# Dividing the attention's output without transposes: sums on sixteen rows of each head

## The chip, the core and the metric

The kernel runs on one core of a Trainium2 chip. The metric is the device time of one execution in microseconds (us); less is better. A core has five engines with a queue of instructions each: TensorE (PE, matmuls and transposes; its weight loads are listed as PEld), VectorE (DVE), ScalarE (ACT), GpSimd (POOL) and SyncE (SP, which here only starts DMA transfers). Each engine works through its queue in order. TensorE writes to PSUM, a memory of eight banks with 128 partitions of 2 KB each (512 numbers of 32 bits); VectorE and ScalarE read PSUM and write to the on-chip memory SBUF or back to PSUM.

## The reference, cut to what matters

The model has two layers on x of 8 batches x 256 tokens x 256 features: a correlation attention, a mixture of experts with balanced assignment, a cross attention, and a mixture with two experts per token. The change is in the cross attention and in what follows it at once:

```
q = (x @ Wq + bq).reshape(bs, n_ctx, HEADS, d)
kv = (data @ Wkv + bkv).reshape(bs, n_data, HEADS, 2 * d)
k, v = (kv[..., :d], kv[..., d:])
scores = jnp.einsum('bqhd,bkhd->bhqk', q, k) * scale
attn = jax.nn.softmax(scores, axis=-1)
out = jnp.einsum('bhqk,bkhd->bqhd', attn, v).reshape(bs, n_ctx, WIDTH)
return out @ Wp + bp
...
x = x + _L1_xattn_ref(_layernorm(x, axis=-1), ctx_1024, L1_xattn_Wq, ...)
x = x + _L1_ffn_ref(_layernorm(x, axis=-1), L1_ffn_gate_W, ...)
```

The softmax is computed as exponents first, sums of the exponents beside the product with v, and a division at the end.

## The kernel before, in words

Everything is in 32-bit floats. The program order of every engine's queue is written out by hand: what `fast_path` calls first is first in the queues. Work of several batches is interleaved, so that TensorE always has something to do.

**The attention stage** (`for b in range(B): for c in range(NB):`, L3018 to L3107) runs over 8 batches b and two halves c of 8 heads. Per half it issues `scores` for two tiles of 128 keys (L2666): four matmuls of 32 rows each, one per pair of heads, where `QM` holds the queries of a pair twice, once with the first head's features kept and once with the second's (m = 0, 1). Two exponents on ScalarE follow (L2681). `values` (L2685) then multiplies the exponents of the half before (`prev`) with `VA`: for each head a block of 32 columns, 16 of v, one of ones, 15 of zeros. So each head has 32 rows of the result `pv`: 16 features, one row with the sum of the exponents, 15 of nothing.

From there to the projection there are five steps. `keep` (L2698) copies pv to SBUF on VectorE. `turn_back` (L2702) turns both halves of a batch with eight transposes on TensorE, so that tokens lie on partitions and the sum of a head is a column; VectorE takes the reciprocal of 16 sums per token and multiplies (L2717, L2718). `turn_out` (L2725) turns the normalised output back with four transposes, and VectorE copies it (L2735). `project_out` (L2737) multiplies with Wp and VectorE adds to X (L2749).

Around it: `turn_q` (L2628) turns the normalised rows of the next batch but one, VectorE copies them (`hT`); `queries` (L2632) computes the queries of a batch in two halves c, each with its own PSUM tile `pp`, and makes the two masked copies m with the mask `mask[:, m]`: m = 0 on ScalarE, m = 1 on VectorE. `norm_q` normalises the rows for turn_q, `batch_stats` takes mean and variance (VectorE, with a power on POOL), `add_y` adds the expert output of the layer before, `add_bias` runs on POOL. For the mixture that follows, the rows of batch b-2 are normalised by POOL (`norm_m`) and turned: for batches 0 to 5 by `take_apart_m` (ScalarE splits the numbers into 16-bit halves, two DMA transposes on SP's queue turn them) and `join_m` (ScalarE), for the last two batches by `turn_m` (four transposes on TensorE, a copy on ScalarE). The router (`route`, L2843) is a generator, advanced step by step from batch 4 on by `next(gates)`; its small products (`pl`, `pt`, `pc`) use the same PSUM tiles.

PSUM in this stage: the pool `ps_m` has three tiles of one bank, used in turn by pt, pp, pl and pc; `ps_s` has two tiles of two banks for scores; `ps_v` has one bank for pv. A tile that comes round again waits until the last reader of its former content is done.

After the loop (L3767 to L3827) the last values, turn_back, turn_out and project_out are placed between pieces of the shared expert's first matmuls (`classic_up`, L3237). From L3885 on the mixture runs in units of a seven-product scheme, whose sums of operands (`Rows.steps`, four VectorE operations) are placed at fixed points of `run_unit` (`early`, `amid`, `late`, `after`).

Of the kernel before, what the change touches and what calls it, by code (L numbers as in the profile page):

```python
# [9 lines left out]
F32 = mybir.dt.float32  # L10
# [1076 lines left out]
def fast_path(  # L1087
# [263 lines left out]
    KT = pk.tile([P, NB, T], F32, name="KT")  # L1351
    VA = pk.tile([P, NT, H, HW], F32, name="VA")
    WK = pst.tile([P, KC, H, DH], F32, name="WK")
# [61 lines left out]
    def vals(i, n, pool, copy=nc.scalar.copy):  # L1415
        pp = pool.tile([P, n, H, DH], F32, tag="pm", name="pp")
        for j in range(n):
            for kc in range(KC):
                nc.tensor.matmul(
                    pp[:, j],  # L1420
                    CT[:, kc, (i + j) * P : (i + j + 1) * P],
                    wkv[:, kc, :, 1, :],
                    start=(kc == 0),
                    stop=(kc == KC - 1),
                )
                if kc < KC - 1 or j < n - 1:
                    yield
        copy(VA[:, i : i + n, :, 0:DH], pp)
        yield
# [65 lines left out]
    nc.vector.tensor_copy(bsel, fold.to_broadcast([P, NCT, 16]))  # L1495
    nc.gpsimd.memset(VA[:, :, :, DH:], 0.0)
    nc.gpsimd.memset(VA[:, :, :, DH : DH + 1], 1.0)

# [965 lines left out]
    for e in range(E - 1):  # L2464
        if e == 5:

            wpv = L1_xattn_Wp.rearrange("(c g m d) n -> m g d c n", c=NB, g=4, m=2)
            for m in range(2):
                for g in range(4):
                    r0 = 64 * m + DH * g  # L2470
                    nc.sync.dma_start(out=wp[r0 : r0 + DH], in_=wpv[m, g])
                    nc.sync.dma_start(
                        out=bvc[r0 : r0 + DH, :],
                        in_=bkv[:, 1, :].rearrange("(c g m) d -> m g d c", c=NB, g=4)[m, g],
                    )
            nc.sync.dma_start(out=bpb, in_=L1_xattn_bp.partition_broadcast(P))
        search(
            e, rows.get(e), steps_of(e), *FILLS.get(e, (2.58, [2.58] * 4))
        )
        if e < 2:  # L2480
            for k, _ in enumerate(listers[e]):
                fill((1.29, 0.43, 1.72, 0.43)[k])
# [59 lines left out]
    banks = ctx.enter_context(ExitStack())  # L2542
    ps_m = banks.enter_context(tc.tile_pool(name="ps_m", bufs=3, space=PSUM))
    ps_s = banks.enter_context(tc.tile_pool(name="ps_s", bufs=2, space=PSUM))
    ps_v = banks.enter_context(tc.tile_pool(name="ps_v", bufs=1, space=PSUM))
    pq2 = at.enter_context(tc.tile_pool(name="pq2", bufs=2))
# [15 lines left out]

    QM, hTs, h2s, norms = {}, {}, {}, {}

# [67 lines left out]
    def queries(b, c, eng=nc.scalar):  # L2632
        if c == 0:
            QM[b] = pq2.tile([P, NB, 2, S], F32, tag="QM", name="QM")
        pp = ps_m.tile([P, S], F32, tag="pm", name="pp")
        for kc in range(KC):
# [7 lines left out]
        for m in range(2):  # L2644
            if m == 0 and eng is nc.scalar:
                nc.scalar.activation(
# [16 lines left out]
    pex = at.enter_context(tc.tile_pool(name="pex", bufs=4))  # L2663
    ex, pvs, ovs, ons, oTs = {}, {}, {}, {}, {}

# [19 lines left out]
    def values(b, c, m):  # L2685
        if m == 0:
            pvs[b, c] = ps_v.tile([P, 2, S], F32, tag="pv", name="pv")
        for kt in range(TPB):
            for g in range(4):
                nc.tensor.matmul(  # L2690
                    pvs[b, c][32 * g : 32 * g + 32, m, :],
                    VA[:, b * TPB + kt, 8 * c + 2 * g + m, :],
                    ex[b, c, kt][:, g, m, :],
                    start=(kt == 0),
                    stop=(kt == TPB - 1),
                )

    def keep(b, c):  # L2698
        ovs[b, c] = pxs.tile([P, 2, S], F32, tag="ov", name="ov", bufs=3)
        nc.vector.tensor_copy(ovs[b, c], pvs.pop((b, c)))  # L2700

    def turn_back(b):  # L2702

        on = pxs.tile([P, TPB, NB, 2, 4, DH], F32, tag="on", name="on")
        ons[b] = on
        for qt in range(TPB):
            pt = ps_m.tile([P, NB, 2, 4, HW], F32, tag="pm", name="pt")
            for c in range(NB):
                for m in range(2):
                    nc.tensor.transpose(  # L2710
                        pt[:, c, m].rearrange("p g w -> p (g w)"),
                        ovs[b, c][:, m, qt * P : (qt + 1) * P],
                        ident,
                    )
            pv = pt.rearrange("p c m g w -> p (c m g) w")
            rs = small.tile([P, H, 1], F32, tag="rs", name="rs")
            nc.vector.reciprocal(rs, pv[:, :, DH : DH + 1])  # L2717
            nc.vector.tensor_tensor(  # L2718
                on[:, qt].rearrange("p c m g d -> p (c m g) d"),
                pv[:, :, 0:DH],  # L2720
                rs.to_broadcast([P, H, DH]),
                ALU.mult,
            )

    def turn_out(b):  # L2725
        pt = ps_m.tile([P, NB, TPB, P], F32, tag="pm", name="pt")
        for c in range(NB):
            for qt in range(TPB):
                nc.tensor.transpose(
                    pt[:, c, qt, :],  # L2730
                    ons[b][:, qt, c].rearrange("p m g d -> p (m g d)"),
                    ident,
                )
        oTs[b] = pxs.tile([P, NB, TPB, P], F32, tag="oT", name="oT")
        nc.vector.tensor_copy(oTs[b], pt)  # L2735

    def project_out(b):  # L2737
        pp = ps_m.tile([P, TPB, D], F32, tag="pm", name="pp")
        for qt in range(TPB):
            for c in range(NB):  # L2740
                nc.tensor.matmul(
                    pp[:, qt, :],
                    oTs[b][:, c, qt, :],
                    wp[:, c, :],
# [12 lines left out]
    def turn_m(b):  # L2757
# [3 lines left out]
            nc.scalar.copy,  # L2761
        )

    def between_m(b, kc):
        return HT[:, kc, (b + 1) * S : (b + 3) * S].bitcast(U16)

    def take_apart_m(b):  # L2770
        parts = between_m(b, 0)
        nc.scalar.copy(
            parts.rearrange("p (r t d) -> p r t d", r=TPB, t=2),
            HP[:, TPB * b : TPB * (b + 1), 0:D]
            .bitcast(U16)
            .rearrange("p r (d t) -> p r t d", t=2),
        )
        turned = between_m(b, 1).rearrange("p (c q) -> p c q", q=S)
        for r in range(TPB):
            nc.sync.dma_start_transpose(  # L2780
                out=turned[:, :, r * P : (r + 1) * P],
                in_=parts[:, 2 * D * r : 2 * D * (r + 1)],
            )

    def join_m(b):
        nc.scalar.copy(
            HT[:, :, b * S : (b + 1) * S]
            .bitcast(U16)
            .rearrange("p k (q t) -> p k q t", t=2),
            between_m(b, 1).rearrange("p (t k q) -> p k q t", t=2, k=KC),  # L2790
        )
# [226 lines left out]
    for b in range(B):  # L3018
        for c in range(NB):
# [4 lines left out]
            if (b, c) == (3, 0):  # L3024
                router_weights()
            if prev:
                values(*prev, 0)
                values(*prev, 1)
                keep(*prev)
            send()  # L3030
            if prev is None:
                list(vals(4, 1, ps_m, nc.vector.tensor_copy))
            elif b == 0:
                turn_q(1)
            elif c == 0:
                if b + 1 < B:
                    turn_q(b + 1)
            else:
                turn_out(b - 1)
                if b >= 2:  # L3040
                    take_apart_m(b - 2)
            if c == 0 and b >= 3:
                join_m(b - 3)
            if gates:
# [14 lines left out]
            if c == 0:  # L3059
                if b >= 1:  # L3060
                    turn_back(b - 1)
                if 0 < b and b + 1 < B:
# [705 lines left out]
    values(*prev, 1)  # L3768
    keep(*prev)
    join_m(B - 3)  # L3770
    at.close()
# [6 lines left out]
    next(up0)  # L3778
    turn_back(B - 1)
    gate2 = route(2)  # L3780
    next(gate2)
    next(up0)
    turn_out(B - 1)
    next(gate2)
# [3 lines left out]
    norm_m(B - 1)  # L3788
    send(2)
    next(gate2)  # L3790
    turn_m(B - 2)
# [34 lines left out]
    for do in shared.steps(P, HF):  # L3826
# [6 lines left out]
        for i in range(2)  # L3833
    ]
    ps_a = ctx.enter_context(tc.tile_pool(name="ps_a", bufs=2, space=PSUM))
    ps_e = ctx.enter_context(tc.tile_pool(name="ps_e", bufs=2, space=PSUM))
    ps_m = ctx.enter_context(tc.tile_pool(name="ps_m", bufs=1, space=PSUM))
    ps_v = ctx.enter_context(tc.tile_pool(name="ps_v", bufs=1, space=PSUM))
# [47 lines left out]
    for b in range(NBLK):  # L3886
# [24 lines left out]
        for k in range(1, NK):  # L3911
# [18 lines left out]
            if b == 1 and k == 3:  # L3930
                t = turned[n]
                early, amid = [lambda: t.join(0)], [lambda: t.join(1)]
                xs_[n] = Rows(t.RT)
                after = xs_[n].steps()
            if b == 2 and k == 1:
                amid = [lambda: t.join(0), lambda: t.join(1)]
                xs_[n] = Rows(t.RT)
            if b == 2 and k == 2:
                late = xs_[n].steps()
            run_unit(up_unit(b, k), early, amid, late, after)  # L3940
# [72 lines left out]
```

## Time and profile before

| what | us |
|---|---|
| median of 3 runs | 808.18 (807.61 to 808.23) |
| the profiled execution | 807.99 |
| its span, first to last instruction | 806.3 |
| TensorE busy in the span | 790.3 (98%) |
| mean granted TensorE clock | 0.997 |
| attention stage (205 to 360): PE, DVE, ACT, POOL busy of 155 | 152.1, 98.4, 97.5, 72.7 |

The profile is of one execution. A group line names the line of the code, the engine, the operation, the output and inputs by their names in the program, and how often it ran. The timeline gives start and duration in us; in brackets stands the time for which the engine had been idle and the instruction that released it. "Busy" of TensorE has modelled ends, so consecutive groups overlap by some hundredths in the timeline; the time from one start to the next is what a piece of work takes in the queue.

### The profile page before, as it was taken

Reading aid. Unit: us, or ns where it says so; the run is one execution under the profiler, and the core shown is the slowest. Engines: PE = TensorE matmul, PEld = TensorE weight load, DVE = VectorE, ACT = ScalarE, POOL = GpSimd, SP = SyncE. Lnnn points to the kernel's source line nnn. Section 1 sums busy time; section 2 is a strip of 40 time slices with the busy share of each in tenths; the row PEclk is TensorE's granted clock in tenths of the full one; section 3 lists DMA queues with packets and bytes.
Section 4 is the critical chain, followed back from the end, with each engine's and each line's share of the span. In section 5 each row is a group of like instructions: output and inputs, shape, how many; then the busy total and the mean of one; then the engine's idle time right before and its main releaser. Section 6 shows DMA issues by size and latency. Waiting matters only on the chain. (4 is left out here: it accounts for less than half of the span.)

```text
span 806.3 us, 13762 instructions
## 1 busy us (share of the span) xinstructions
PE 790.3 (98%) x5100; PEld 627.6 (78%) x5100; DVE 521.1 (65%) x1473; ACT 369.6 (46%) x676; POOL 214.2 (27%) x293
## 2 busy tenths in 40 slices
PE   7999999999999999999999999999999999999997
PEld 6547778788755555547898989798979898999996
DVE  6367887640466686456866686767676859686732
ACT  4344455234367777531425364444444535433430
POOL 6343122231126546543230001102122311112030
PEclk9999999999999999999999999999999999999999
DMA  8292666596161102161113585797759554411023
GB/s 267 78 307 86 218 202 174 191 269 224 53 182 30 27 16 59 41 210 60 56 55 100 170 243 156 190 298 197 196 137 296 111 179 112 122 14 20 8 30 132
DMA packets 111252, 111.16 MB, mean 138 GB/s; under 512 B 32936, under 2 KB 101768, under 8 KB 111144
## 3 DMA queue, kind: packets, MB, share of 16 engines
q1 hardware_dynamic: 102504, 96.87, 39.9%
q0 software_dynamic: 7920, 13.02, 7.6%
q8 instruction: 42, 0.69, 0.4%
q10 hardware_dynamic: 752, 0.30, 0.1%
q14 instruction: 34, 0.28, 0.1%
HBM read 80.61 MB, written 25.37 MB: 131 GB/s over the span
## 5 line engine op out<-in xcount | busy, mean ns | idle before, releaser
L3589 POOL DMA_INDIRECT Od<-Y,ids x32 | 50.7, 1584 | 285.1 <-DVE Y L3414 100.0
L3274 ACT COPY B<-a 128x512 f32<-128x512 f32 (+1 forms) x54 | 28.6, 531 | 168.2 <-PE a L3286 132.2
L2681 ACT ACTIVATE ex<-p,scale 128x1024 f32<-128x1024 f32 x64 | 67.8, 1110 | 25.3 <-PE p L2673 24.5
L3286 PE MATMUL a<-T,HP 128*128 128x256 f32 x288 | 73.9, 379 | 0.0
L3136 DVE TENSOR_TENSOR cc<-e,s 128x512 f32<-128x512 f32 x44 | 30.4, 691 | 57.1 <-PE e L3286 57.0
L3286 PE MATMUL a<-RT,wab 128*128 128x256 f32 x256 | 66.4, 382 | 0.4 <-DVE cc L3136 0.4
L3136 DVE TENSOR_TENSOR act<-act 128x256 f32<-128x256 f32 (+1 forms) x120 | 61.5, 513 | 2.7
L2385 PE MATMUL ph<-RT,w 128*128 128x256 f32 x256 | 62.0, 390 | 0.0
L2402 PE MATMUL py<-w,A 128*128 128x256 f32 x256 | 61.6, 387 | 0.0
L3286 PEld LDWEIGHTS a<-T,HP 128*128 128x128 f32 x288 | 54.0, 190 | 7.0
L3286 PEld LDWEIGHTS a<-RT,wab 128*128 128x128 f32 x256 | 46.5, 190 | 8.1 <-issue 1.6
L2385 PEld LDWEIGHTS ph<-RT,w 128*128 128x128 f32 x256 | 45.1, 190 | 8.0 <-ACT RT L2370 0.5
L2402 PEld LDWEIGHTS py<-w,A 128*128 128x128 f32 x256 | 46.3, 190 | 6.1
L2394 ACT ACTIVATE A<-ph,b1c 128x256 f32<-128x256 f32 x64 | 30.3, 474 | 43.7 <-PE ph L2385 36.7
L2944 POOL DMA_INDIRECT Td<-HP,to x32 | 32.6, 1017 | 59.5 <-DMA Td<-HP,to 54.1
L2673 PE MATMUL p<-QM,KT 32*128 32x512 f32 x256 | 41.0, 639 | 1.0 <-DVE QM L2654 0.5
L3136 DVE TENSOR_TENSOR act<-act,cc 128x512 f32<-128x512 f32 x44 | 30.3, 689 | 13.2 <-ACT act L3320 13.0
L2412 POOL DMA_INDIRECT Yd<-Y,ids x16 | 15.8, 988 | 74.5 <-DVE Y L2411 22.5
L3301 ACT COPY s<-a 128x512 f32<-128x512 f32 x44 | 25.8, 587 | 20.0 <-PE a L3286 20.0
L3286 PE MATMUL e<-T,wab 128*128 128x256 f32 x128 | 32.9, 380 | 0.3 <-DVE T L3136 0.3
L3136 DVE TENSOR_TENSOR cc<-a,s 128x512 f32<-128x512 f32 x44 | 30.4, 691 | 3.9
L3286 PE MATMUL B<-RT,wab 128*128 128x256 f32 x128 | 32.9, 379 | 0.0
(522 smaller groups left out, 1732.4 us busy)
## 6 DMA issues: line engine op xcount, KB each, us to landing
w<-in_L_ffn_w_dram SPq DMA_DIRECT2D x16, 1024.0 KB
wab<-in_L_ffn_w_e_dram SPq DMA_DIRECT2D x16, 1024.0 KB
wc<-in_L_ffn_w_e_dram SPq DMA_DIRECT2D x8, 1024.0 KB
sab<-in_L_ffn_w_e_dram SPq DMA_DIRECT2D x32, 256.0 KB
R<-Td SPq DMA_DIRECT2D x8, 530.0 KB
sc<-in_L_ffn_w_e_dram SPq DMA_DIRECT2D x16, 256.0 KB
Td<-blank SPq DMA_DIRECT2D x2, 1590.0 KB
X<-in_x_dram SPq DMA_DIRECT2D x4, 512.0 KB
```

The costliest lines, as they stand in the source:

```text
L2385: nc.tensor.matmul(ph, w1[:, kc, f * P : (f + 1) * P], RT[:, kc, :], start=(kc == 0), stop=(kc == KC - 1),)
L2394: nc.scalar.activation(A[:, f, :], ph, AF.Gelu_apprx_tanh, bias=b1c[:, e, f : f + 1])
L2402: nc.tensor.matmul(py, A[:, f, r * P : (r + 1) * P], w2[:, f, :], start=(f == 0), stop=(f == NF - 1),)
L2412: nc.gpsimd.indirect_dma_start(out=Yd, out_offset=bass.IndirectOffsetOnAxis(ap=ids[:, r : r + 1], axis=0), in_=Y[:, r, :], in_offset=None,)
L2673: nc.tensor.matmul(ps[g // 2][:, g % 2].rearrange("p m q -> p (m q)"), KT[rows, c, k0 : k0 + P], QM[b][rows, c].rearrange("p m q -> p (m q)"),
L2681: nc.scalar.activation(e4[:, 2 * j : 2 * j + 2], ps[j], AF.Exp, scale=scale)
L2944: nc.gpsimd.indirect_dma_start(out=Td, out_offset=bass.IndirectOffsetOnAxis(ap=to[g][:, k, j : j + 1], axis=0), in_=HP[:, GT * g + j, :], ...
L3136: eng.tensor_tensor(out, a, b, op)
L3274: nc.scalar.copy(self.b[:, 0 : self.n], self.a[:, 0 : self.n])
L3286: nc.tensor.matmul(ps[:, m * HT2 : (m + 1) * HT2], self.w.get(m, left, self.k), self.x.part[right], start=start and m == 0, stop=True, ski ...
L3301: nc.scalar.copy(self.s2, self.a)
L3589: nc.gpsimd.indirect_dma_start(out=Od, out_offset=bass.IndirectOffsetOnAxis(ap=ids, axis=0), in_=Y, in_offset=None, compute_op=ALU.add,)
```

## The change

`VA` now holds, for each pair of heads, four blocks of 16 columns: v of the first head, ones, ones, v of the second. `values` takes blocks 0 and 1 for m = 0 and blocks 2 and 3 for m = 1. So in the 32 rows of a pair, pv[:, 0] has the first head's features on rows 0 to 15 and its sum on each of rows 16 to 31; pv[:, 1] has the second head's sum on rows 0 to 15 and its features on rows 16 to 31. keep, turn_back and turn_out are gone; `divide` takes their place: it gathers the sums in `den`, swaps the 16-row halves, inverts, gathers the features in pv[:, 0], and multiplies. Its result already has features on partitions, as project_out needs them; the rows of Wp are loaded in the new order.

pv comes from `ps_m`, which has two tiles now; `ps_s` has three. The two halves of a batch's queries share one tile. Of the four masked copies ScalarE makes three (both of c = 1). turn_q stands ahead of values. The mixture's rows of all batches go through `turn_m`, at half c = 1 of the second next batch; `take_apart_m` and `join_m` are gone. Some sums of `Rows` are placed later, and the pools of the last stage are opened in another order.

```
-    VA = pk.tile([P, NT, H, HW], F32, name="VA")
+    VA = pk.tile([P, NT, H // 2, 4, DH], F32, name="VA")
...
-    nc.gpsimd.memset(VA[:, :, :, DH:], 0.0)
-    nc.gpsimd.memset(VA[:, :, :, DH : DH + 1], 1.0)
+    nc.gpsimd.memset(VA[:, :, :, 1:3, :], 1.0)
...
-                    r0 = 64 * m + DH * g
+                    r0 = 2 * DH * g + DH * m
...
-    ps_m = banks.enter_context(tc.tile_pool(name="ps_m", bufs=3, space=PSUM))
-    ps_s = banks.enter_context(tc.tile_pool(name="ps_s", bufs=2, space=PSUM))
-    ps_v = banks.enter_context(tc.tile_pool(name="ps_v", bufs=1, space=PSUM))
+    ps_m = banks.enter_context(tc.tile_pool(name="ps_m", bufs=2, space=PSUM))
+    ps_s = banks.enter_context(tc.tile_pool(name="ps_s", bufs=3, space=PSUM))
...
     def queries(b, c, eng=nc.scalar):
         if c == 0:
             QM[b] = pq2.tile([P, NB, 2, S], F32, tag="QM", name="QM")
-        pp = ps_m.tile([P, S], F32, tag="pm", name="pp")
+            pqs[b] = ps_m.tile([P, NB, S], F32, tag="pm", name="pp")
+        pp = pqs[b][:, c]
...
-            if m == 0 and eng is nc.scalar:
+            if eng is nc.scalar and (m == 0 or c == 1):
...
+    held = mask.bitcast(U32)
+    swap = list(range(DH, 2 * DH)) + list(range(DH))
...
-            pvs[b, c] = ps_v.tile([P, 2, S], F32, tag="pv", name="pv")
+            pvs[b, c] = ps_m.tile([P, 2, S], F32, tag="pm", name="pv")
...
-                    VA[:, b * TPB + kt, 8 * c + 2 * g + m, :],
+                    VA[:, b * TPB + kt, 4 * c + g, 2 * m : 2 * m + 2, :],
...
+    def divide(b, c):
+        if c == 0:
+            oTs[b] = pxs.tile([P, NB, S], F32, tag="oT", name="oT")
+        pv = pvs.pop((b, c))
+        den = pxs.tile([P, S], F32, tag="den", name="den")
+
+        def upper(m):
+            return held[:, m : m + 1].to_broadcast([P, S])
+
+        nc.vector.tensor_copy(den, pv[:, 0])
+        nc.vector.copy_predicated(den, upper(0), pv[:, 1])
+        nc.vector.stream_shuffle(den, den, swap)
+        nc.vector.reciprocal(den, den)
+        nc.vector.copy_predicated(pv[:, 0], upper(1), pv[:, 1])
+        nc.vector.tensor_tensor(oTs[b][:, c], pv[:, 0], den, ALU.mult)
...
+            if c == 0 and 0 < b < B - 1:
+                turn_q(b + 1)
             if prev:
                 values(*prev, 0)
                 values(*prev, 1)
-                keep(*prev)
+                divide(*prev)
             send()
             if prev is None:
                 list(vals(4, 1, ps_m, nc.vector.tensor_copy))
             elif b == 0:
                 turn_q(1)
-            elif c == 0:
-                if b + 1 < B:
-                    turn_q(b + 1)
-            else:
-                turn_out(b - 1)
-                if b >= 2:
-                    take_apart_m(b - 2)
-            if c == 0 and b >= 3:
-                join_m(b - 3)
+            elif c == 1 and b >= 2:
+                turn_m(b - 2)
...
             if c == 0:
-                if b >= 1:
-                    turn_back(b - 1)
                 if 0 < b and b + 1 < B:
                     queries(b + 1, 0)
                     queries(b + 1, 1)
...
-    keep(*prev)
-    join_m(B - 3)
+    divide(*prev)
...
-    turn_back(B - 1)
     gate2 = route(2)
-    next(gate2)
-    next(up0)
-    turn_out(B - 1)
     next(gate2)
     next(up0)
     project_out(B - 1)
...
-                after = xs_[n].steps()
+                sums = xs_[n].steps()
+                late, after = sums[:1], sums[1:]
...
-                late = xs_[n].steps()
+                sums = xs_[n].steps()
+            if b == 2 and k >= 2:
+                after = after + sums[2 * k - 4 : 2 * k - 2]
```

More of the change, by code (lines that the diff above doesn't have):

```diff
@@ L1427, in vals @@
                     yield
-        copy(VA[:, i : i + n, :, 0:DH], pp)
+        copy(
+            VA[:, i : i + n, :, 0:4:3, :],
+            pp.rearrange("p n (g m) d -> p n g m d", m=2),
+        )
         yield
@@ L2561, in fast_path @@
     load_y(2)
-    QM, hTs, h2s, norms = {}, {}, {}, {}
+    QM, hTs, h2s, norms, pqs = {}, {}, {}, {}, {}
     def add_y(b):
@@ L2663, in fast_path @@
     pex = at.enter_context(tc.tile_pool(name="pex", bufs=4))
-    ex, pvs, ovs, ons, oTs = {}, {}, {}, {}, {}
+    ex, pvs, oTs = {}, {}, {}
+    held = mask.bitcast(U32)
+    swap = list(range(DH, 2 * DH)) + list(range(DH))
     def scores(b, c, kt):
@@ L2696, in values @@
                 )
[L2698 to L2735, printed above, removed]
+    def divide(b, c):
[11 more added lines that the diff above has]
+        nc.vector.tensor_tensor(oTs[b][:, c], pv[:, 0], den, ALU.mult)
     def project_out(b):
@@ L2742, in project_out @@
                     pp[:, qt, :],
-                    oTs[b][:, c, qt, :],
+                    oTs[b][:, c, qt * P : (qt + 1) * P],
                     wp[:, c, :],
@@ L2761, in turn_m @@
             nc.scalar.copy,
[L2762 to L2790, printed above, removed]
         )
@@ L3789, in fast_path @@
     send(2)
+    next(gate2)
+    next(up0)
     next(gate2)
@@ L3834, in fast_path @@
     ]
+    ps_m = ctx.enter_context(tc.tile_pool(name="ps_m", bufs=1, space=PSUM))
+    ps_e = ctx.enter_context(tc.tile_pool(name="ps_e", bufs=2, space=PSUM))
     ps_a = ctx.enter_context(tc.tile_pool(name="ps_a", bufs=2, space=PSUM))
-    ps_e = ctx.enter_context(tc.tile_pool(name="ps_e", bufs=2, space=PSUM))
-    ps_m = ctx.enter_context(tc.tile_pool(name="ps_m", bufs=1, space=PSUM))
     ps_v = ctx.enter_context(tc.tile_pool(name="ps_v", bufs=1, space=PSUM))
```

## The prediction

> **What bounds the kernel now.** I read the page's first part, then the busy time by stretch, then TensorE's timeline inside the stretch that the change touches, then the single rows that price the new instructions.
>
> ```profile
> PE 790.3 (98%) x5100; PEld 627.6 (78%) x5100; DVE 521.1 (65%) x1473; ACT 369.6 (46%) x676; POOL 214.2 (27%) x293
> ```
> ```profile
> 205.00:360.00 155.00, 152.11 (x1208) 85.67 (x1207) 98.44 (x309) 97.46 (x106) 72.72 (x121) 1.00 0.27 78
> ```
> TensorE (PE) is the bound everywhere: 98% of the span, and 152.1 of the 155 us from 205 to 360, the attention stage, where the edits lie. There VectorE (DVE) has 98 us of work and ScalarE (ACT) 97 us. So work taken from PE is worth its full time, if nothing makes PE wait. One batch (b=3) on PE:
>
> ```profile
> 258.71 1.54 PE L2673 MATMUL p<-QM,KT 32*128 32x512 f32 x8
> ...
> 260.18 1.93 PE L2690 MATMUL pv<-ex,VA 128*32 128x256 f32 x32
> 262.04 0.66 PE L2619 MATMUL pt<-ident,h 128*128 128x128 f32 x4
> 262.63 1.14 PE L2673 MATMUL p<-QM,KT 32*128 32x512 f32 x8
> 263.70 1.09 PE L2710 MATMUL pt<-ident,ov 128*128 128x128 f32 x8
> 264.63 1.89 PE L2637 MATMUL pp<-hT,wq 128*128 128x256 f32 x8
> 266.45 1.14 PE L2673 MATMUL p<-QM,KT 32*128 32x512 f32 x8
> 267.52 1.93 PE L2690 MATMUL pv<-ex,VA 128*32 128x256 f32 x32
> 269.39 0.65 PE L2729 MATMUL pt<-ident,on 128*128 128x128 f32 x4
> 269.97 1.14 PE L2673 MATMUL p<-QM,KT 32*128 32x512 f32 x8
> 271.04 1.99 PE L2741 MATMUL pp<-wp,oT 128*128 128x256 f32 x8
> 272.97 1.48 PE L2673 MATMUL p<-QM,KT 32*128 32x512 f32 x8
> ```
> The columns are start, time from first to last, engine, line. From start to start, the slots are: scores 1.07, values 1.87, four transposes 0.58, turn_back 0.93, queries 1.82 to 1.93 (each half 0.95), project_out 1.93. The first scores of a batch take 1.41 to 1.47, since they wait some 0.37 for ScalarE. Half c=0 takes 7.74 us (258.71 to 266.45), half c=1 6.52, a batch 14.26.
>
> **What goes.** Per batch PE loses turn_back (0.93) and turn_out (0.58), gains turn_m's transposes (0.58), and with three score buffers loses the 0.37. With no wait, c=0 is then 1.07+0.58+1.87+1.07+1.90 = 6.49 (1.25 less) and c=1 is 1.07+1.87+0.58+1.07+1.93 = 6.52, as before. That is all there is to win: 8 x 1.25 and 1.4 in the tail (0.96+0.44 at 337 and 342 us), 11 us. ScalarE loses 1.05+1.16 (take_apart_m, join_m), gains 0.59 and 0.57 a batch: off the path. The transposing DMAs leave SP's queue, where nobody on PE waited for them. The shorter memset (0.53 us of POOL at 4.8 us) and the order of the Rows sums in a stretch where PE is 99.7% busy (149.55 of 150 us from 450 to 600) I cost at nothing, within 0.5 us either way: DVE has 30% of idle there. If that cover failed, one 0.42 us sum would be late per step.
>
> **What comes: `divide`, six VectorE operations in a row.** The price rests on these rows (min/median/max ns):
>
> ```profile
> L1803 DVE RECIPROCAL rtot<-es x1: 159/159/159, 35.8 to 35.8; 128x1 f32<-128x1 f32 x1
> L2876 DVE RECIPROCAL rsm<-sm x4: 177/178/178, 286.4 to 365.9; 128x4 f32<-128x4 f32 x4
> L2717 DVE RECIPROCAL rs<-pt x16: 247/250/258, 235.9 to 340.3; 128x16 f32<-128x16 f32 x16
> ```
> ```profile
> L2718 DVE TENSOR_TENSOR on<-pt,rs x16: 424/425/425, 236.2 to 340.6; 128x256 f32<-128x256 f32 x16
> ```
> A reciprocal grows by (250-159)/15 = 6.1 ns for each element of a row, and by 6.3 between the first two rows, while the product of 256 elements takes only 425 ns in all. The old code inverted one sum per head and query (16 elements a row); the new one inverts 256, sixteen copies of each sum: 159 + 255 x 6.07 = 1.71 us. The Trainium skill's page "VectorE: DVE Perf Modes", section "First, the fixed hardware budget", has the reciprocal repeat its divide step 8 times at 0.96 GHz, an estimate of 2.28 us by that page; the rows here give 6 and not 8.3 ns, and I take the rows. By the page each wait below would be 0.57 longer and the sum some 9 us larger.
>
> The rest: copy from PSUM 0.425 (row of G<-pg); two predicated copies, which no row shows, 0.42 each by the product's row (lower end: a one-element operation, 0.15; upper: a 512-element one, 0.69); the shuffle 0.42 as a copy and 0.08 for loading its pattern, as MATCH_VALUE_LOAD has (ends 0.15 and 0.77); the product 0.425. Between dependent operations the trace shows 0.04 (rs at 264.39 for 0.26, on at 264.69). With the second predicated copy overlapping a little, the chain is 0.465+0.46+0.54+1.71+0.42+0.425 = **4.02 us**. Ends: reciprocal at a plain 0.42, 2.73, and with the unknown operations at their lower ends too, about 1.9; reciprocal at the slope from 178 to 258 ns (6.7), 1.86, and the unknown ones at their upper ends, 5.0. VectorE's work per batch goes from about 9.7 (two thirds of 14.26 in the same windows) to 13.8: it loses keep 2 x 0.69, reciprocals and products 2 x 0.68, oT 0.68 and a mask 0.54, and gains 8.04. DVE starts 0.14 after PE's slot ends (values ends at 262.04, ov starts at 262.18), and PE starts about 0.1 after DVE (oT ends 256.64, project_out starts 256.78).
>
> **First new wait: the buffer of `pv`.** Before, `keep` emptied pv in 0.69 us, and pv had a bank of its own. Now pv stays in use until the product, and pv, the transposes, queries and project_out share two buffers in turn. In c=1 the order is pv, pt (turn_m), pp (project_out), so pp takes pv's buffer: project_out waits for the whole divide of the same half. Beside it PE has only 0.58+1.07. c=1 = 1.07+1.87+(0.14+4.02+0.10)+1.93 = **9.13** for 6.52. Behind the waiting matmul stands all of PE.
>
> **Second new wait: the bank of the queries.** Both halves of a batch's queries now lie in one bank. In this trace a bank is entered by one engine at a time, even for reads, and for different halves:
>
> ```profile
> 265.81 0.57 ACT L2646 ACTIVATE QM<-pp,bqm,mask 128x256 f32<-128x256 f32 x1
> 266.41 0.54 DVE L2654 TENSOR_SCALAR QM<-pp,mask,bqm 128x256 f32<-128x256 f32 x1 [0.68 <-ACT QM L2646]
> ```
> ```profile
> 23.11 0.47 ACT L1594 ACTIVATE qk<-pqk,bqc 128x256 f32<-128x256 f32 x1 [0.66 <-PE pqk L1445]
> 23.62 0.43 DVE L1596 TENSOR_TENSOR qk<-pqk,Rq 128x256 f32<-128x256 f32 x1 [2.74 <-ACT qk L1594]
> ```
> So I expect the matmuls of queries c=1 to wait for both masks of c=0. The second of these is the one that stays on DVE, and it is queued behind divide. ScalarE's is done earlier: exponents from 1.17 to 3.3 after the scores start, mask to 3.9. c=0 = 1.07+0.58+1.87+(0.14+4.02+0.05+0.54+0.10)+0.95 = **9.32** for 7.74. No row shows a matmul held by a read of the other half; if there is none, this half is 6.49, and a wait for DVE moves to the next half (DVE's loop from divide through project_out, X's sum, two statistics, the copy of hT, divide, mask and X's next sum is about 16.2 us a batch).
>
> **The sum**, batch by batch against the slots of the trace: before the loop queries(0) wait for their masks, +1.0. b=0: after values, hT's copy stands behind divide (4.88), then two masks on DVE between the two query halves, 8.15 for 3.97: +4.2. b=1: 10.3 (turn_q now ahead of values waits 1.0 for its normalised rows) and 9.13 for 13.87: +5.5. b=2 and 3: 18.45 for 14.26, +8.4. b=4 and 6 (the router's logits add 0.57; its transpose takes pv's buffer, so the wait comes ahead of the scores): 9.89+10.4 for 14.88, +5.4 each. b=5: the router's counts wait for its picks behind divide, then the masks for its sums: 11.9+9.1 for 15.42, +5.6. b=7: 17.2 for 13.39, +3.8. Tail -1.4. Together **+37.9 us**. The profiled execution took 807.99 us, its span 806.3 and 1.7 around it; 0.2 under the median of 808.18. 807.99+37.9 = **846 us**.
>
> **Rivals.**
> - A cheap reciprocal: if the slope ended at 16 elements, divide is 2.73. c=1 falls to 7.84; c=0 only to 9.07, since ScalarE's mask is then what comes late. By the same table +24: 832 us. The three rows on one slope speak against it.
> - No wait inside the bank: c=0 runs through, but pv's wait and DVE's loop stay, 16.2 a batch, less in b=0, 1: +23, 831 us. For it: no row of such a wait; against: the four rows above.
> - The clock. One row shows the granted clock at half without the load being gone:
>
> ```profile
> 40.00:44.00 4.00, 3.53 (x11) 2.65 (x12) 1.35 (x9) 0.00 (x0) 0.00 (x0) 0.57 0.99 364
> ```
> There thin matmuls and a wait of 0.95 us were followed by some 3 us at 0.50; a wait of 1.49 us at 8.6 us left it at 1.00. My waits are 2.6 to 3.8 us. If each of about 15 brings 3 us at half clock, 1.5 us more each, +23: 869 us. The skill's page "TensorE: Matmul & The Clock Gate", section "Why this matters for your kernels", warns of idle gaps over about 3 us; by it the two longest waits alone would count, an estimate of 3 us in all.
> - Faster: the mechanism is PE's saved 1.25 us in c=0, and it decides where the queries don't wait in their bank and divide is under 2.66 us: then 6.49+(1.07+1.87+2.66+0.24+1.93) = 14.26, even with before. At 1.4 us, where PE's own 1.65 covers it, 11 us are won: 797 us. It needs the low end of the unknown rows and a reciprocal against its three rows.
>
> **Chances.** Forecast as worked out (840 to 861 by divide from 3.6 to 5.0, about 15 waits) 0.62; no wait in the bank 0.12; clock 0.10; cheap reciprocal 0.09; a wash 0.03; faster 0.04. The range takes in the first, second and fourth: 826 to 862, leaving out 0.17. A measurement of this kernel tells 0.2% from no change: faster 0.04, same 0.03, slower 0.93.
>
> **What would show it.** Reciprocal of 128x256 near 1.71 us; in the chain of waits, project_out (pp) behind the product of divide for about 2.6 us, seven or eight times; the queries behind DVE's QM mask, about 2.8 us; PE's busy share in the attention stage down to some 75%, the stage some 38 us longer, and the mixture stage as long as before. If project_out starts right after the scores, pv is freed sooner than I think; if the queries run 1.9 us unbroken, the bank isn't kept for one engine; if the reciprocal is near 0.4 us, the slope was wrong.

## The result and the profile after

The changed kernel takes **854.7 us** (median of 6, 851.4 to 855.7) against 808.2 (median of 6, 807.0 to 809.3): 1.0572 times as long, interval 1.0559 to 1.0585, or 46.5 us more. The forecast was 846, 37.9 us more. Its profiled execution has a span of 852.6 us, a mean granted clock of 0.968 (before 0.997) and a TensorE that is busy 94% of the time (98%).

The busy time by stretch of the kernel after (start, end, length, then PE, PEld, DVE, ACT, POOL with the number of instructions, granted clock, DMA share and GB/s; the first row is the window of the prediction, 205 to 360, the second the whole attention stage):

```profile
205.00:360.00 155.00, 122.01 (x884) 60.94 (x882) 98.28 (x253) 71.94 (x83) 52.14 (x92) 0.86 0.13 38
209.49:378.93 169.44, 131.92 (x981) 64.10 (x979) 111.52 (x297) 83.23 (x95) 58.28 (x102) 0.86 0.13 38
```

The same stretch of work of the kernel before, from the small matmuls ahead of the attention stage (pbp) to the last values:

```profile
209.83:331.55 121.72, 118.83 (x1042) 66.65 (x1040) 82.52 (x253) 87.16 (x93) 57.45 (x101) 1.00 0.24 63
```

All of the loss is in this stretch: 169.4 us for 121.7, **+47.7**. From the last values to the end of the span there are 473.7 us, for 474.8 before. In the stretch TensorE idles 37.5 us for 2.9, so 34.6 of the 47.7 us are waits. The other 13.1 are busy time, and that although 0.9 us of transposes a batch have gone net (1.51 less, 0.58 more): the same matmuls ran slower, at a granted clock of 0.86 for 1.00.

VectorE's new work has the size that was forecast. Groups of the kernel after in the attention stage (busy us, mean ns | idle before, releaser):

```profile
L2716 DVE RECIPROCAL den<-den 128x256 f32<-128x256 f32 x16 | 28.0, 1753 | 0.6
L2714 DVE COPY_PREDICATED den<-mask,pv 128x256 f32<-128x256 uint32 x16 | 7.1, 443 | 0.6
L2715 DVE STREAM_SHUFFLE den<-den 128x256 f32<-128x256 f32 x16 | 7.0, 436 | 0.0
L2717 DVE COPY_PREDICATED pv<-mask,pv 128x256 f32<-128x256 uint32 x16 | 6.5, 407 | 0.0
```

One batch (b=2) on PE, then on DVE, from its timeline:

```profile
259.40 1.14 PE L2677 MATMUL p<-QM,KT 32*128 32x512 f32 x8
...
264.74 1.13 PE L2639 MATMUL pp<-hT,wq 128*128 128x256 f32 x4
268.27 1.49 PE L2639 MATMUL pp<-hT,wq 128*128 128x256 f32 x4 [2.40 <-DVE QM L2656]
269.69 2.09 PE L2677 MATMUL p<-QM,KT 32*128 32x512 f32 x8
271.71 2.20 PE L2694 MATMUL pv<-ex,VA 128*32 128x256 f32 x32
...
275.50 1.99 PE L2724 MATMUL pp<-wp,oT 128*128 128x256 f32 x8
```
```profile
263.81 0.42 DVE L2713 COPY den<-pv 128x256 f32<-128x256 f32 x1
...
267.34 0.42 DVE L2718 TENSOR_TENSOR oT<-pv,den 128x256 f32<-128x256 f32 x1
267.68 0.53 DVE L2656 TENSOR_SCALAR QM<-pp,mask,bqm 128x256 f32<-128x256 f32 x1
...
277.52 0.43 DVE L2718 TENSOR_TENSOR oT<-pv,den 128x256 f32<-128x256 f32 x1
```

Three things are to be seen. `divide` lasts from 263.81 to 267.76, 3.95 us. The second half of the queries (268.27) waits 2.40 us for VectorE's mask, which is queued behind divide, and then takes 1.42 us from start to start, for 0.95 before; the next scores take 2.02 for 1.07. And project_out starts at 275.50, while the divide of the same half ends only at 277.95: the wait that was forecast there isn't there.

TensorE's five largest waits in the stretch of the kernel after (us in total, times, longest; at `pc` the router's counts wait for its picks `mk`, at `pt` a transpose waits for the router's turned weights `gwT`):

```profile
PE pp L2639 <- DVE QM L2656: 15.6, 8, 2.4
PE pc L2856 <- DVE mk L2852: 7.2, 2, 3.7
PE pp L2639 <- DVE hT L2623: 3.0, 1, 3.0
PE pp L2724 <- DVE oT L2718: 2.8, 2, 1.4
PE pt L2620 <- DVE gwT L2793: 2.0, 1, 2.0
```

### The profile page after: what moved, and what is told of

It reads as the page before. It is cut to its first block, busy times and chain, and to the rows that moved or that the text cites. A ratio compares the mean times of both kernels' runs of the same rounds, so it can differ in the third digit from the quotient of the medians.

```text
span 852.6 us, 13649 instructions
## 1 busy us (share of the span) xinstructions
PE 802.0 (94%) x5028; PEld 623.6 (73%) x5028; DVE 551.6 (65%) x1522; ACT 363.6 (43%) x677; POOL 216.0 (25%) x292
## 4 chain that ended last, share of the span: by engine, by line
PE 85%; DVE 10%; DMA 2%; ACT 1%; issue 1%; ACTq 0%; SPq 0%; DVEq 0%
PE a L3233 18%; PE e L3233 9%; PE a L3292 8%; PE ph L2387 7%; PE py L2404 7%; PE B L3233 4%; PE e L3292 4%; PE pv L2694 4%; PE py L3438 3%; PE pgu L3195 3%; DVE den L2716 3%; PE p L2677 3%; PE pp L2639 2%; PE B L3292 2%; PE pp L1419 2%; PE pp L1398 2%
## 5 line engine op out<-in xcount | busy, mean ns | idle before, releaser
L2677 PE MATMUL p<-QM,KT 32*128 32x512 f32 x256 | 44.0, 759 | 0.0
L2639 PE MATMUL pp<-hT,wq 128*128 128x256 f32 x64 | 24.5, 519 | 19.7 <-DVE QM L2656 15.6
L3083 DVE TENSOR_TENSOR act<-act,cc 128x512 f32<-128x512 f32 x44 | 30.3, 688 | 13.3 <-ACT act L3267 13.1
L2694 PE MATMUL pv<-ex,VA 128*32 128x256 f32 x512 | 36.7, 435 | 1.6 <-DVE X L2732 1.1
L2639 PEld LDWEIGHTS pp<-hT,wq 128*128 128x128 f32 x64 | 13.9, 240 | 30.8 <-DVE QM L2656 19.7
L2414 POOL DMA_INDIRECT Yd<-Y,ids x16 | 16.3, 1019 | 75.7 <-DVE Y L2413 21.6
L2694 PEld LDWEIGHTS pv<-ex,VA 128*32 128x32 f32 x512 | 16.6, 123 | 25.5 <-issue 14.1
```

What stands on the lines that cost most here:

```text
L2639: nc.tensor.matmul(pp, wq[:, kc, c * P : (c + 1) * P], hTs[b][:, kc, :], start=(kc == 0), stop=(kc == KC - 1),)
L2677: nc.tensor.matmul(ps[g // 2][:, g % 2].rearrange("p m q -> p (m q)"), KT[rows, c, k0 : k0 + P], QM[b][rows, c].rearrange("p m q -> p (m q)"),
L2694: nc.tensor.matmul(pvs[b, c][32 * g : 32 * g + 32, m, :], VA[:, b * TPB + kt, 4 * c + g, 2 * m : 2 * m + 2, :], ex[b, c, kt][:, g, m, :], ...
L3083: eng.tensor_tensor(out, a, b, op)
```

## The experiments

My theory (1): the second half of the queries waits in the shared bank for the masks of the first, and the clock falls behind each such wait. Rivals: VectorE's length itself (2), the two ps_m tiles (3), a clock that follows something else (4). The table has all runs; "stretch" is from pbp to the last values in the profiled execution, waits are TensorE's in it, all in us.

| kernel | us | stretch | waits |
|---|---|---|---|
| before | 807 to 808 | 121.7 | 2.8 |
| after | 854.7 | 169.4 | 37.1 |
| a_first: query matmuls ahead of the masks | 833.5 | 149.1 | 28.0 |
| c_pools: tiles of before, queries share one | 854.1 | 166.1 | 31.9 |
| b_sep: tiles of before, queries apart | 828.3 | 139.5 | 16.3 |
| d_sep2: two ps_m tiles, queries apart | 841.8 | 155.9 | 31.9 |
| e_norecip: copy for the reciprocal | (3534) | 150.2 | 28.3 |
| g_s2: two score tiles | 855.1 | 171.4 | 34.8 |
| f_warm: g_s2, nine matmuls in the wait | 854.3 | 168.7 | 22.1 |
| f_warm5: g_s2, five matmuls in the wait | 845.2 | 163.3 | 23.8 |
| j_order: divide at the end of the half | 835.3 | 146.0 | 23.4 |
| l_gates: b_sep, router and hT ahead of divide | 812.5 | 129.1 | 11.6 |
| m_late: l_gates, router's counts later | 818.1 | 128.5 | 11.8 |
| n_scalar: m_late, hT by ScalarE | 817.9 | 127.8 | 9.7 |

**a_first**

```
                 stop=(kc == KC - 1),
             )
-        for m in range(2):
+        if c == 0:
+            return
+        for c, m in [(c, m) for c in range(NB) for m in range(2)]:
+            pp = pqs[b][:, c]
```

> The changed kernel with one edit: all eight matmuls of a batch's queries come ahead of the four masked copies; the shared tile, the two ps_m tiles and divide stay. Theory 1 (the second half's matmuls wait in the shared bank for the copies of the first, 2.4 us a batch, and the clock falls after it): these waits go (15.6 us from 205 to 400, some 3 before the loop), the granted clock of the stage rises from 0.86 to 0.95 or more, and with it some 12 us: 820 to 830 us for 854.7. Theory 2 (VectorE is too long with its 1.75 us reciprocal, whoever waits for it): the wait moves to the next step that needs VectorE, and no more than 8 us are won, 846 or above.

833.5 us (827.8 to 838.6), ratio to before 1.0322 (1.026 to 1.0383): 21 us less than after, a little short of theory 1 and far from theory 2. Batch 2 on PE now has full speed throughout:

```profile
260.52 1.99 PE L2639 MATMUL pp<-hT,wq 128*128 128x256 f32 x8
262.44 1.14 PE L2680 MATMUL p<-QM,KT 32*128 32x512 f32 x8
263.60 1.93 PE L2697 MATMUL pv<-ex,VA 128*32 128x256 f32 x32
```

Its divide still runs, from 259.59 to 263.46, beside these matmuls, and none of them waits for it. This batch takes 13.98 us (255.54 to 269.52), 18.03 in the kernel after and 14.26 in the one before.

**c_pools and b_sep.** Both have `ps_m` 3, `ps_s` 2 and pv in `ps_v`; b_sep also has

```
-            pqs[b] = ps_m.tile([P, NB, S], F32, tag="pm", name="pp")
-        pp = pqs[b][:, c]
+        pp = ps_m.tile([P, S], F32, tag="pm", name="pp")
```

> As the kernel with the tiles of before, but both halves of the queries share one tile as in the change. Theory 1 (shared bank): queries wait 2.4 us a batch for VectorE's mask as in the changed kernel; 850 to 858, within some 4 us of it. Theory 3 (two ps_m tiles too few): as fast as the kernel with the tiles of before, 830 or below. Theory 2: no difference to either.

> The changed kernel with the PSUM tiles of before: three of ps_m, two of ps_s, one of pv's own, and a tile for each half of the queries. The order of work and divide stay. Theory 1 (shared bank): the wait of 2.4 us goes, as in the run with the matmuls first, pv's wait of 2.8 us in all goes too, and 0.37 a batch comes back at the first scores, 3 us: 820 to 830. Theory 2 (length of VectorE's work): 846 or above. Theory 3 (only two ps_m tiles are too few): 820 to 830 as well, and then the next kernel, which has these pools and keeps the shared tile, is as fast.

854.1 us (1.0569, 1.0536 to 1.0602) and 828.3 (1.0263, 1.0246 to 1.028). The tiles of before alone bring nothing that the median shows; theory 3 falls. The stretch of c_pools is 3.3 us shorter than after, but the part behind the stretch is 5 us longer in both kernels (478.7 and 478.5 for 473.7): there `turn_m` waits some 3 us for rows that POOL normalises, and the shared expert's next matmuls take 5.2 us for 3.5; the same is so in j_order and n_scalar, and in m_late the part is 3 us longer. The shared tile costs 26 us. In c_pools the wait stands as it was, in b_sep it is gone (the largest of c_pools, then the two largest of b_sep):

```profile
PE pp L2640 <- DVE QM L2657: 16.2, 8, 2.7
```
```profile
PE pc L2856 <- DVE mk L2852: 7.1, 2, 3.6
PE p L2677 <- ACT ex L2685: 3.9, 2, 2.0
```

The Trainium skill's page "PSUM — Partial Sum Buffer", section "PSUM bank collisions raise a hardware error", says that two engines must not work on the same bank and partitions at once, disjoint columns included, and that software has to order them. These two runs agree: with both halves in one bank there are 16.2 us of waits, in banks of their own none. As tile and bank change together in them, they don't tell whether the order is kept for the bank or for the tile.

**d_sep2** (the edit of b_sep on the two ps_m tiles of the change)

> The changed kernel with a tile for each half of the queries again, but only the two ps_m tiles of the change. Theory 1 (bank, and the first wait of the prediction in another place): the second half takes pv's tile and waits for the end of divide, which is 0.5 us before the end of VectorE's mask; 848 to 853. Rival (the shared tile alone is at fault, two tiles are enough): like the run with the matmuls first, 828 to 838.

841.8 us (1.0419, 1.0401 to 1.0437), between the ranges of theory and rival. The second half now takes pv's tile in five batches and waits for the product of divide:

```profile
PE pp L2638 <- DVE oT L2717: 10.2, 5, 2.0
```

So the wait for pv's buffer exists as a mechanism; in the change project_out meets it in two batches only.

**e_norecip** (`nc.vector.tensor_copy(den, den)` for the reciprocal: the sums are not inverted). The flags at the program's end then start its general path as well, hence the 3534 us; only the stretch is read.

> The changed kernel with a plain copy in the place of the reciprocal, so it leaves out the inversion and multiplies by the sums. It prices 1.75 against some 0.42 us, 1.33 less in each of 16 divides. Theory 1: the queries then wait for ScalarE's mask instead, which is done 0.75 us earlier than VectorE's now; so 0.8 us less wait a batch, 6 us, and as much again if the clock falls less: 840 to 849. Theory 2 (the length of divide is the cost, 16 times): 21 us less at the least, 834 or below.

The stretch is 150.2 us, 19.2 less than after: nearer to the 21 that the length of divide (2) asked for than to my 12. But not by the wait that I had priced. In batch 2:

```profile
254.94 2.12 ACT L2685 ACTIVATE ex<-p,scale 128x1024 f32<-128x1024 f32 x2 [1.40 <-PE p L2677]
...
255.92 0.42 DVE L2718 TENSOR_TENSOR oT<-pv,den 128x256 f32<-128x256 f32 x1
256.95 0.56 ACT L2648 ACTIVATE QM<-pp,bqm,mask 128x256 f32<-128x256 f32 x1
257.55 0.54 DVE L2656 TENSOR_SCALAR QM<-pp,mask,bqm 128x256 f32<-128x256 f32 x1 [1.21 <-ACT QM L2648]
258.14 1.44 PE L2639 MATMUL pp<-hT,wq 128*128 128x256 f32 x4 [2.24 <-DVE QM L2656]
```

VectorE is done at 256.34 and stands idle 1.21 us; ScalarE's exponents come first, then its mask, and only then VectorE's, out of the same bank. The wait is still 2.24 us. So VectorE's mask is the one named, but without it ScalarE would hold the bank nearly as long; of the 1.46 us that divide became shorter this wait got 0.16. The rest of the gain is at the other waits behind divide (mk 7.2 to 4.6, hT 3.0 to 1.6, oT 3.3 to 0) and in the clock (0.86 to 0.92 from 205 to 360).

**g_s2, f_warm and f_warm5.** g_s2 has `ps_s` with two tiles; the others also work through the wait inside the queries of batches 2 to 7, on a bank of their own:

```
+        if c == 0 and b >= 2:
+            for _ in range(5):
+                nc.tensor.matmul(
+                    fill, wq[:, 0, 0:P], hTs[b][:, 0, :], start=True, stop=True
+                )
```

(f_warm has 9 for 5.)

> The changed kernel with two score tiles for three (ps_s), nothing else. It leaves a bank free and is the partner of the next run. Prediction's term: 0.37 us come back at the first scores of each batch, 3 us: 856 to 859. Rival: where TensorE waits elsewhere anyway, ScalarE is up to date at the first scores and nothing comes back: 853 to 856.

> As the run with two score tiles, but nine matmuls on a bank of their own (9 x 0.24 us, results unused) stand between the two halves of the queries for batches 2 to 7, so TensorE works through the 2.4 us in which it waits. It adds work and takes no wait away. Theory of the clock (the wait of 2.4 us is what brings the half clock after it, some 0.5 in the second half of the queries and 1.0 in the scores behind): 8 to 12 us less than the run without them, and the granted clock of the stage up from 0.87 to 0.92 or more. Rival (the clock follows something else): within 2 us of it, or longer by what the nine overshoot.

> As the run with nine matmuls between the halves of the queries, but five. There a matmul of 256 columns took 0.43 us and not 0.24, since it is issued in two passes, so nine lasted 3.9 us and overshot the end of the wait by 1.3 us a batch, about what the full clock behind them gave back. Five last some 2.15, less than the wait of 2.4. Theory of the clock: the second half of the queries and the scores behind take 2.03 instead of 3.5 us in six batches, and the matmuls end 0.2 to 0.3 us ahead of the mask: 7 to 9 us less than the run without them, 846 to 848. Rival (the clock follows something else): within 2 us of it, 853 to 857.

g_s2: 855.1 us (1.058, 1.0562 to 1.0598), as after (854.7): the third score tile brings nothing here. f_warm: 854.3 (1.057, 1.0553 to 1.0588), within 1 us of it, so by its own expectation a point for the rival; its trace showed that nine matmuls last 3.9 us, longer than the wait, and that I had mis-sized them. f_warm5: **845.2** (1.0468, 1.0449 to 1.0486), 9.9 us less than g_s2 (9.0 by the two ratios, since the runs were on different chips), with added work and no mask that comes earlier. Batch 2 of g_s2, then of f_warm5:

```profile
266.12 1.57 PE L2639 MATMUL pp<-hT,wq 128*128 128x256 f32 x4 [2.39 <-DVE QM L2656]
267.62 2.09 PE L2677 MATMUL p<-QM,KT 32*128 32x512 f32 x8
269.64 2.13 PE L2694 MATMUL pv<-ex,VA 128*32 128x256 f32 x32
271.70 0.66 PE L2620 MATMUL pt<-ident,HP 128*128 128x128 f32 x4
```
```profile
263.46 2.32 PE L2650 MATMUL fill<-hT,wq 128*128 128x256 f32 x10
266.02 1.13 PE L2641 MATMUL pp<-hT,wq 128*128 128x256 f32 x4 [0.23 <-DVE QM L2663]
267.08 1.14 PE L2684 MATMUL p<-QM,KT 32*128 32x512 f32 x8
268.15 1.93 PE L2701 MATMUL pv<-ex,VA 128*32 128x256 f32 x32
270.01 0.66 PE L2622 MATMUL pt<-ident,HP 128*128 128x128 f32 x4
```

From the start of the second half to the transposes: 5.58 us without the filling, 3.99 with it. So idling in the wait is what brings the slow matmuls behind it. The price is not the same each time: from the first half of the queries to the end of the values behind them, the six filled places become 1.6, 1.6, 3.1, 1.5, 0.2 and −0.3 us shorter (7.6 of the 8.1 us by which the stretch is shorter). In the last one g_s2, too, ran at full speed behind its wait of 2.40 us; in the one before it, the five matmuls themselves ran slowly and overshot.

**j_order** (pv in two tiles of its own, two score tiles, a_first's order of the matmuls with VectorE's mask last, ScalarE's masks for batch 1, `divide` called at the end of each half, turn_q(1) ahead of values)

> The kernel with pv in tiles of its own (two) and two tiles each of ps_m and ps_s, with all query matmuls ahead of the masks, and divide issued at the end of each half, behind the copy of hT, the router's steps and the masks of ScalarE; turn_q(1) ahead of values. VectorE does the same work in another order. Theory 1 continued (what is left over the kernel before is work queued behind divide: hT of batch 1, the router's mk and exponents, 10 to 14 us of waits and the clock after them): batches of 13.0 to 13.8 us, 798 to 808 in all. Rival (VectorE's length itself, 13.8 us of work a batch and more with the router, is the bound): 815 to 828, with waits spread over other tiles.

835.3 us (1.034, 1.0323 to 1.0358): outside the ranges of theory and rival. In batch 2 divide stands behind `h`, which waits 1.9 us for POOL, and the next hT behind divide:

```profile
251.67 0.73 DVE L2597 TENSOR_SCALAR h<-X,b_mv,b_r 128x256 f32<-128x256 f32 x2 [1.92 <-POOL b_r L2591]
252.33 0.41 DVE L2717 COPY den<-pv 128x256 f32<-128x256 f32 x1
...
258.19 0.68 DVE L2624 COPY hT<-pt 128x512 f32<-128x512 f32 x1
```

TensorE waited 2.2 us for this hT. My reading is that VectorE isn't short of time here but 4 us late in the wrong place; no run separates the two.

**l_gates, m_late and n_scalar.** l_gates is b_sep with `divide` behind the half's first `next(gates)`, turn_q(1) ahead of values, and ScalarE's masks for batch 1. m_late adds two `yield` ahead of the router's counts, n_scalar also copies hT on ScalarE.

> The kernel with the tiles of before and a tile for each half of the queries, and three pieces of VectorE's queue put ahead of divide: the router's first step of a half (so mk, and the shifted logits that ScalarE's exponents wait for), and hT of batch 1 (turn_q(1) ahead of values); the masks of batch 1 go to ScalarE as those of the other batches. Theory 1 continued (what is left is work queued behind divide): mk's 7.1 us of wait fall to 1 or 2, the scores' 3.9 to 0, hT's 3.0 to 1, and the granted clock from 280 to 360 rises from 0.89 to 0.96 or more; 808 to 816. Rival (any place of a 4 us divide makes something else late, as in the run with divide at the end of each half): 822 or above.

> The kernel of the last run but with the router's counts (pc) two steps of its generator later, so that TensorE meets them after the values of the next half and not before the queries. There TensorE still waited 5.1 us for mk in two places, with some 4 us at half clock behind them. Theory 1 continued: both go; 803 to 808. Rival (VectorE runs behind in batches 5 and 7, with the router's 4 us beside two divides, whoever asks): the wait moves to pv, hT or the masks: 809 to 813.

> As the run with the counts later, and ScalarE copies hT (0.58 us) in the place of VectorE (0.68), so that divide stands that much earlier in VectorE's queue in every batch. Theory of VectorE's lag: the 2.5 us in which the values of batch 7 wait for divide shrink, and the times fall by 1 to 3 us against the run with the counts later: 801 to 806. Rival (ScalarE, with 8.5 us of exponents, three masks and HT in a batch of 13.6, becomes late for the scores or the queries): 2 us or more above it.

l_gates: **812.5 us** (811.7 to 820.1), ratio to before 1.0088 (1.0061 to 1.0115), 42 us less than after and still a little slower than before. Batches 1 to 3 take 13.3 to 13.8 us, for 13.9 to 14.3 before; batches 5 and 7, with the router, take 18.5 and 18.4 us, for 15.4 and 13.4 before: there TensorE waits for VectorE. m_late has 818.1 (1.013, 1.0113 to 1.0147) and n_scalar 817.9 (1.0124, 1.0102 to 1.0146); both lie outside the ranges of theory and rival. The waits for mk in l_gates (first fence) are gone in m_late (second, for its whole span), and others stand in their place, as m_late's rival had it:

```profile
PE pc L2856 <- DVE mk L2852: 5.1, 2, 3.1
PE pv L2694 <- DVE oT L2718: 2.5, 1, 2.5
```
```profile
PE pv L2694 <- DVE oT L2718: 4.1, 3, 2.5
PE pp L2639 <- DVE hT L2624: 3.7, 2, 2.5
PE pt L2621 <- POOL HP L2597: 2.9, 2, 2.0
```

The stretch of m_late is as long as that of l_gates (128.5 and 129.1), and the part behind it is longer (476.8 for 473.8), since turn_m waits there for POOL's normalised rows. Whether the length of VectorE's work is the bound in batches 5 and 7 is not shown: n_scalar takes 4 us of it out of the stretch (103.8 us busy for 107.9), and the stretch becomes only 0.7 us shorter. No version beat the kernel before.

## Why the prediction was right, and where not

The time lay in the forecast range, 8.6 us above the forecast, and the sum was made up otherwise than I had written.

- **divide, 4.02 us**: measured 3.95. The reciprocal at 1.71 by the slope of three rows: 1.753. The unknown operations at 0.42 and 0.50: 0.443, 0.407 and 0.436 with 0.014 for the pattern. By the Trainium skill's page "VectorE: DVE Perf Modes", section "First, the fixed hardware budget", the reciprocal had been an estimate of 2.28 us; the trace, with 1.753, decides for the rows.
- **Second wait, in the bank, 2.8 us a batch**: it is there, eight times: 2.25 to 2.41 us in five, 1.09 to 1.37 in three, among them the one ahead of the loop. c_pools against b_sep shows that sharing the tile, and with it the bank, is the cause. ScalarE's mask is done at 267.47 in batch 2, only 0.74 before VectorE's, so a shorter divide wins little at this wait. The rival of the cheap reciprocal had said so (9.07 for 9.32), and e_norecip shows it (2.24 for 2.40).
- **First wait, "pp takes pv's buffer", 2.6 us a batch**: this is the step that failed. I took the two tiles to be used in strict turn. project_out starts 2.45 us before pv is free in batch 2 and waits in two batches only, 1.4 us each: 2.8 us for some 20. Half c=1 of batch 2 took 7.74 us for the 9.13 forecast, and its 1.2 us over 6.52 are not this wait but scores and values at the lower clock. Where it waits, it is for oT, as forecast. That the pool gives out the tile that comes free first is my reading of the starts; no run was made for it.
- **The clock**, a rival at 0.10 that I had left out of the sum, took its place. That idling brings the half clock is shown by f_warm5 (9.9 us from six filled waits). For the whole stretch I estimate 20 us: 131.9 us busy after, and about 112 of work, from l_gates's 117.4 at a clock of 0.96 (129.1 x 0.04 x 2 = 10 us at half speed, half of it lost). The rival's price of 1.5 us for a wait fits three of those six (1.5 to 1.6; one was 3.1, two about nothing), and its sum of 23 is near my estimate; as the clock came instead of the first wait and not beside it, the time wasn't 869. TensorE's busy share from 205 to 360 was 79% (122.0 of 155) for the 75% forecast, as slow matmuls count as busy.
- **Luck**: the total came out so near because two errors nearly cancel, some 18 us of first wait that weren't there and some 20 us of clock that weren't in the sum.
- **The router**: I gave 5.4 to 5.6 us to batches 4 to 6; they took 5.5, 6.6 and 4.7 more. Batch 3 was forecast at 4.2 and took 8.7 more: I had left out that the router's weights, too, stand on VectorE's queue behind divide (2.0 us for gwT, and 0.4 for X); the values and scores behind that wait took 1.6 us more than at full clock. Batch 0 took 5.7 more for the 4.2 forecast; batches 1, 2 and 7 took 4.8, 3.8 and 3.2 for 5.5, 4.2 and 3.8.
- **Ahead of the loop, +1.0**: 4.8. Waits are 2.6 us longer, 1.35 of it for VA, since vals, too, now has two tiles only (in c_pools, with three, it doesn't wait for VA); most of the rest is the clock.
- **Tail −1.4 and a mixture as long as before**: −1.1, right.
- **0.37 a batch for the third score tile**: not seen in the time (g_s2 against after, 0.4 in all). In g_s2 the first scores of batch 4 do take 1.47 again, for 1.07 after, but waits behind them become shorter.
- **Faster, if the queries don't wait**: it asked for divide under 2.66 us as well. a_first shows that at 3.95 us an ordinary batch is already below before's (13.98 for 14.26). What kept l_gates behind is batch 0 (1.2 us over before) and the router's batches, with the clock behind their waits.

## What to carry to other kernels

Work moved from a full engine to one with idle time is free only where nothing that the full engine waits for is queued behind it: write down that queue, item by item, before adding a 4 us piece to it. Give outputs that are read at once banks of their own, or issue all their matmuls ahead of the first reader. Price a wait on TensorE at its length and the half clock that can follow it (here 2.4 us, and most often 1.6 behind it), and look whether useful matmuls can be put into it.

## What the runs showed of the hardware that I had not expected

A wait of 2.4 us was enough to bring the granted clock to 0.61 over the next 4 us (268 to 272 in the kernel after), but not each time: of the five waits of 2.25 to 2.41 us in that kernel four were followed by slow matmuls, and behind this one the clock stood at 1.00 for 4 us (scores 1.07, as before):

```profile
351.66 1.13 PE L2639 MATMUL pp<-hT,wq 128*128 128x256 f32 x4 [2.40 <-DVE QM L2656]
352.72 0.64 PE L2803 MATMUL pl<-HT,gwT 128*32 128x128 f32 x16
353.29 1.14 PE L2677 MATMUL p<-QM,KT 32*128 32x512 f32 x8
354.36 1.93 PE L2694 MATMUL pv<-ex,VA 128*32 128x256 f32 x32
```

What decides between the two isn't shown. Shorter waits can do: behind one of 1.37 us that followed one of 0.77, the queries' second half took 2.01 us for 0.95 (c_pools, ahead of the loop). The Trainium skill's page "TensorE: Matmul & The Clock Gate", section "Why this matters for your kernels", warns of gaps over about 3 us; here shorter ones did it, and the measurement decides. Five matmuls whose results nobody uses, put into each of six waits, made g_s2 9.9 us faster (f_warm5); nine of them won nothing (f_warm).
